# A gate's inner channels turned round on TensorE, and the gate's terms issued in another order, in the first layer of a two-layer image network

## The chip, the cores and the metric

One Trainium2 chip, of which the kernel uses one core. The metric is device time in microseconds (us) of one launch, which computes both layers for the whole batch of eight images. The kernel before takes 14973.04 us, the median of three runs (14967.72 to 14974.38). A core has five engines with instruction queues of their own: TensorE (PE; its weight loads are listed as PEld), VectorE (DVE), ScalarE (ACT), GpSimd (POOL) and SyncE (SP), which here only issues transfers (DMA). The engines work each in the order of its queue and wait for one another through semaphores.

## The reference, cut to what matters

The first layer, in which everything that the change touches lies, is this, for x of 8 images, 128 channels, 128 x 128 points. The second layer (a 3x3 convolution, a small scan over tokens, a group norm) is not touched.

```
feat = gelu(batchnorm(conv2d(x, conv_w, padding=3, dilation=3)))    # 64 channels
F2   = fft2(feat)
q = k = complex_l2_norm(F2 as 8 heads of 8 channels);  v = F2
attn = complex_softmax(einsum(q, conj(k)) * tau)                    # 8x8 per head
out_f = abs(ifft2(attn @ v))
cg   = gelu(batchnorm(conv2d(F2.real, cg1_w) + cg1_b))              # 64 -> MID = 4 channels
cg   = sigmoid(conv2d(cg, cg2_w) + cg2_b)                           # 4 -> 64 channels
gate = abs(ifft2(cg * F2))
x1   = concatenate([out_f, gate], channels) + x
```

Both convolutions of the gate have 1x1 kernels. So cg1_w, which mixes channels, may be applied to feat before the transform instead of to F2.real after it, and that is what the kernel does: it takes the 4 inner channels per image from feat and then transforms only these 4.

## The kernel before, in words

`network` runs `layer0` and then `layer1`. `layer0` goes over the batch in four pairs of images, p = 0 to 3. The 64 channels of image 0 lie on partitions 0 to 63 and those of image 1 on 64 to 127. For each pair it calls `convolve(p)` and then `spectral(p)`. A manual schedule keeps each engine's instructions in the order in which the program issues them.

`convolve` makes 6 rows of feat per group g. `combine(g)` forms sums and differences of input rows (tiles v), mostly on POOL. `block(g)` multiplies them on TensorE into four PSUM tiles m (line 276), which ScalarE copies (`low`, line 282) and VectorE adds up into feat; the Gelu of line 288 finishes the rows. In between, `turn(r)` takes four rows that an earlier group finished. Four transposes (line 307) put them into a PSUM tile tps, of which there are two buffers, and VectorE copies them into fT (line 308), where the 128 columns of the image lie on the partitions. Then four matmuls (line 312) make the gate's inner channels. In each the row of feat, 128 channels by 128 points, is the stationary side, and the moving side is cg1_w with 2 x MID = 8 columns (4 for each image, zero for the other image's channels). The result has the points on the partitions already, as fT has. After 16 rows (CH) VectorE copies 16 x 8 values to mT (line 315). `products(r)` (line 319) adds four rows to the Gram matrix of the softmax.

`spectral` begins with `rows(("m", b), mT, ...)`, `columns` and `hidden(b)`: the transform of the inner channels and their Gelu, kept in hid. After that come NP = 32 steps n of four channels each. For a step, `rows` (line 364) and `columns` (lines 373, 375) transform feat; `gated(n)` (lines 417 to 420, VectorE) multiplies with the gate cg into gp; `columns_back` (lines 427, 428, PSUM tile zps) and `rows_back` (line 436, then Abs, the sum with x on VectorE, and the store) transform back. The gate of step n is made in three parts: `gate_begin(n)`, four ScalarE instructions for the first inner channel (line 395); `gate_end(n)`, three products and three sums for the other inner channels (lines 405 and 408), on VectorE for n < 2 and otherwise on POOL; and `gate_close(n)`, the sigmoid on ScalarE (line 411). Tiles cg have three buffers. `softmax(k)` in three parts turns the Gram matrix into the matrix pT; its part 0 takes a root on ScalarE (line 495), its part 1 a transpose and an exponential (lines 500, 506), its part 2 another transpose (line 512). ScalarE loads a function table whenever it goes to a function of another set. `mixture`, from step 3 on, multiplies feat with pT for the other half of the output.

In the kernel before, the gates of steps 0 and 1 and part 0 of the softmax stand ahead of the loop, and in the loop the gate of step n + 2 is begun. The head of the loop reads:

```
gate_end(0); gate_close(0); softmax(0)
load_mixture(H - CH); load_mixture(H - 2 * CH)
gate_begin(1); gate_end(1)
for n in range(NP + 1):
    if n < NP:
        e = columns(n, 2)
        if n + 2 < NP:
            gate_begin(n + 2)
        gp = gated(n, e)
```

Of the kernel before, what the change touches and what calls it, by code (L numbers as in the profile page):

```python
# [9 lines left out]
F32 = mybir.dt.float32  # L10
# [6 lines left out]
P = 128  # L17
C = 128
H = 128
W = 128  # L20
# [3 lines left out]
MID = 4  # L24
# [117 lines left out]
def layer0(ctx, tc, x, w0, c0, x1):  # L142
# [9 lines left out]
    nc = tc.nc  # L152
# [9 lines left out]
    def cf(name):  # L162
        at, n = C0[name]
        return ct[:, at:at + n]

    def wf(name):
        at, n = W0[name]
        return wt[:, at:at + n]
# [52 lines left out]
        nc.vector.scalar_tensor_tensor(w_mid[:, k], convw[:, 3:6, :], half, w_sum, ALU.mult, ALU.add)  # L221
    w_four = (convw[:, 0:3, :], w_mid[:, 0], w_mid[:, 1], convw[:, 6:9, :])

    def convolve(p):

        with tc.tile_pool(name="l0_x", bufs=2) as xp, \  # L230
                tc.tile_pool(name="l0_v", bufs=1) as vp, \
                tc.tile_pool(name="l0_pc", bufs=1, space=PSUM) as pc, \
                tc.tile_pool(name="l0_pt", bufs=2, space=PSUM) as pt, \
                tc.tile_pool(name="l0_pm", bufs=1, space=PSUM) as pm:
            xins, vs, mps = {}, {}, {}
            FOUR = (1, 2, 0, 3)

            def load(g):

                if g == 0:  # L240
                    xins[0] = first_rows()
                    return
                lo = g * RW - 3
                n = min(RX, H - lo)
                xins[g] = []
                for b in range(2):
                    xt = xp.tile([P, RX, W], F32, name=f"xin{b}")
                    nc.sync.dma_start(xt[:, :n, :], x[2 * p + b, :, lo:lo + n, :])
                    if g < NW and n < RX:
                        nc.gpsimd.memset(xt[:, n:RX, :], 0.0)  # L250
                    xins[g].append(xt)

            def combine(g):
                for j in FOUR:
                    for b in range(2):
                        xt = xins[g][b]
                        v = vs[b, j] = vp.tile([P, 3, W], F32, name=f"v{b}{j}")
                        r0, r1, r2, r3 = (xt[:, 3 * k:3 * k + 3, :] for k in range(4))
                        eng = nc.vector if g == 0 and b == 0 else nc.gpsimd
                        if j == 1:  # L260
                            eng.tensor_add(v, r1, r2)
                        else:
                            eng.tensor_sub(v, *{0: (r0, r2), 2: (r2, r1), 3: (r1, r3)}[j])

            def columns_of(kx):
                dx = (kx - 1) * 3
                return max(0, -dx), min(W, W - dx), dx

            def block(g):
                m = {}  # L270
                for j in FOUR:
                    m[j] = pc.tile([P, 3, W], F32, name=f"m{j}")
                    for kx in (1, 0, 2):
                        wa, wb, dx = columns_of(kx)
                        for b in range(2):
                            nc.tensor.matmul(  # L276
                                m[j][b * CD:(b + 1) * CD, :, wa:wb], w_four[j][:, kx, :],
                                vs[b, j][:, :, wa + dx:wb + dx], start=(kx == 1), stop=(kx == 2))
                r = g * RW
                both = vp.tile([P, 2, 3, W], F32, name="both")  # L280
                low = vp.tile([P, 3, W], F32, name="low")
                nc.scalar.copy(low, m[2])
                nc.vector.tensor_add(both[:, 0], m[1], low)
                nc.vector.tensor_sub(both[:, 1], m[1], low)
                nc.vector.tensor_add(feat[:, r:r + 3, :], m[0], both[:, 0])
                nc.vector.tensor_sub(feat[:, r + 3:r + RW, :], both[:, 1], m[3])
                f = feat[:, r:r + RW, :]
                nc.scalar.activation(f, f, AF.Gelu, bias=bt, scale=bs)

            def rest():  # L290

                r, xt = NW * RW, xins[NW]
                m = pc.tile([P, 3, W], F32, name="m0")
                for ky in (1, 0):
                    for kx in (1, 0, 2):
                        wa, wb, dx = columns_of(kx)
                        for b in range(2):
                            nc.tensor.matmul(
                                m[b * CD:(b + 1) * CD, 0:H - r, wa:wb], convw[:, ky * 3 + kx, :],
                                xt[b][:, 3 * ky:3 * ky + H - r, wa + dx:wb + dx],  # L300
                                start=(ky == 1 and kx == 1), stop=(ky == 0 and kx == 2))
                nc.scalar.activation(feat[:, r:H, :], m[:, 0:H - r, :], AF.Gelu, bias=bt, scale=bs)

            def turn(r):
                tps = pt.tile([P, 4, P], F32, name="tps")
                for j in range(4):
                    nc.tensor.transpose(tps[:, j, :], feat[:, r + j, :], cf("ident"))
                nc.vector.tensor_copy(fT[:, r:r + 4, :], tps)
                if r % CH == 0:
                    mps[0] = pm.tile([P, CH, 2 * MID], F32, name="mps")  # L310
                for j in range(4):
                    nc.tensor.matmul(
                        mps[0][:, r % CH + j, :], feat[:, r + j, :], wf("cg1_w"), start=True, stop=True)
                if r % CH + 4 == CH:
                    nc.vector.tensor_copy(mT[:, r + 4 - CH:r + 4, :], mps[0])

            def products(r):
                for h in range(r, r + 4):
                    nc.tensor.matmul(gram, fT[:, h, :], fT[:, h, :], start=(h == 0), stop=(h == H - 1))

            for g in range(3):
                load(g)
            combine(0)
            turned = summed = 0
            for g in range(NW + 2):
                ready = min(H, g * RW)
                if g < NW:
                    block(g)
                elif g == NW:
                    rest()  # L330
                if g + 1 < NW:
                    combine(g + 1)
                if g + 3 <= NW:
                    load(g + 3)
                fresh = turned
                while turned + 4 <= ready:
                    turn(turned)
                    turned += 4
                while summed < fresh:
                    products(summed)  # L340
                    summed += 4
            while summed < turned:
                products(summed)
                summed += 4

    def spectral(p):

        with tc.tile_pool(name="l0_f1", bufs=1) as f1, \
# [50 lines left out]
            def gate_end(n):  # L399

                b, c = place(n)
                eng = nc.vector if n < 2 else nc.gpsimd
                for m in range(1, MID):
                    t = f2.tile([P, 4, NF], F32, name="cgt")
                    eng.tensor_mul(
                        t, hid[:, b, m:m + 1, :].broadcast_to([P, 4, NF]),
                        w2r[:, c:c + 4, m:m + 1].broadcast_to([P, 4, NF]))
                    eng.tensor_add(cgs[n], cgs[n], t)
# [113 lines left out]
            hidden(1)  # L522
            gate_end(0)
            gate_close(0)
            softmax(0)
            load_mixture(H - CH)
            load_mixture(H - 2 * CH)
            gate_begin(1)
            gate_end(1)
            for n in range(NP + 1):  # L530
                if n < NP:
                    e = columns(n, 2)
                    if n + 2 < NP:
                        gate_begin(n + 2)
                    gp = gated(n, e)
                    if n + 1 < NP:
                        b, c = place(n + 1)
                        rows(n + 1, fT, b * CD + c)
                if n > 0:
                    rows_back(n - 1)  # L540
                if n == NP:
                    break
                if n + 2 < NP:
                    gate_end(n + 2)
                if n >= START:
                    mixture()
                elif n > 0:
                    softmax(n)
                columns_back(n, gp)
                if n + 1 < NP:  # L550
                    gate_close(n + 1)
                if n >= START and n % 2 == 0:
                    mixture()
                roots()
                load_gate(n + 3)
                if n == NP - 5 and 2 * p + 2 < B:
                    first_load(p + 1)
# [603 lines left out]
```

## Time and profile before

| what | value |
|---|---|
| device time, median of three runs | 14973.04 us |
| device time of the profiled execution | 14973.45 us |
| span of the profiled execution | 14971.7 us, mean granted TensorE clock 0.986 |
| layer 0 within the span | about 0 to 2104 us, four pairs at intervals of 525.5 us |
| TensorE busy | 14356.8 us, 96% of the span |
| VectorE, ScalarE, POOL busy | 85%, 55%, 87% of the span |
| line 312, the gate's matmuls | 1024 records for 512 matmuls, mean 247 ns |
| line 307, transposes | 512 records, mean 284 ns |
| line 276, the convolution | 4032 records, about 480 ns |
| line 408 on POOL and on VectorE | 736 and 500 ns |
| line 405 on POOL and on VectorE | 628 and 424 ns |

The page lists busy times over the whole span, six sevenths of which belong to the second layer, so shares of it say little on the first. What follows reads single stretches: a timeline (start, length, engine, line, operation, output and inputs, shapes, count, and in brackets the idle time before it with what ended it), groups of instructions (busy time, mean ns of one, idle time before), and the chain of waits, which is followed back from the end of a stretch to whatever released each step. Ends of matmuls are modelled and overlap the next start, so that the step from start to start is the better price for one in a stream.

### The profile page before, as it was taken

To read this page: it belongs to the slowest core of one execution; us is meant where nothing else is said; L and a number is where in the kernel's file an instruction comes from. 1 tells how busy PE (TensorE), PEld (TensorE's weight loads), DVE (VectorE), ACT (ScalarE), POOL (GpSimd) and SP (SyncE) were. 2 spreads that over 40 slices of the span, in tenths; PEclk is the share of its full clock that TensorE was granted. 3 is DMA by queue.
4 is the path that set the end of the run, shared out by engine and by line. 5 is a ranking of instruction groups with operands and counts; after the bars stand their busy time and mean duration, and the time that the engine had idled before them with its cause. 6 is when DMAs were issued, how large, how long until landed. Compare 5 with 4: busy or idle time off the path is not lost.

```text
span 14971.7 us, 202160 instructions
## 1 busy us (share of the span) xinstructions
PE 14356.8 (96%) x71336; PEld 5692.1 (38%) x71336; DVE 12692.5 (85%) x12439; ACT 8275.3 (55%) x9202; POOL 12962.2 (87%) x7052
## 2 busy tenths in 40 slices
PE   9999999999999999999999999999999999999996
PEld 6676663333333333333333333333333333333332
DVE  3343359999999999999999999999999999999995
ACT  2354255555555555555555555555565555556553
POOL 5655659998999999999999999999999999999996
PEclk9999999999999999999999999999999999999996
DMA  3444456666666666666666666666666666666665
GB/s 126 148 121 119 128 119 121 119 119 118 129 138 133 137 131 137 136 133 134 133 138 134 135 133 134 138 134 135 133 135 138 131 136 134 136 133 135 136 133 138
DMA packets 1091891, 1976.10 MB, mean 132 GB/s; under 512 B 125760, under 2 KB 256832, under 8 KB 1082688
## 3 DMA queue, kind: packets, MB, share of 16 engines
q1 hardware_dynamic: 1090304, 1960.82, 60.7%
q8 instruction: 568, 9.31, 0.3%
q14 instruction: 443, 3.63, 0.1%
q10 hardware_dynamic: 576, 2.35, 0.0%
HBM read 419.16 MB, written 201.33 MB: 41 GB/s over the span
## 4 chain that ended last, share of the span: by engine, by line
PE 73%; DVE 18%; issue 4%; ACT 3%; DMA 1%; POOL 0%; DVEq 0%; SPq 0%; POOLq 0%; ACTq 0%
PE da L781 19%; PE yps L847 9%; PE ups L781 7%; PE pm L134 7%; DVE da L812 6%; PE m L276 4%; DVE h L820 4%; DVE h L796 4%; PE yps L853 4%; PE pm L733 4%; PE pm L866 3%; PE pm L745 3%; DVE hc L831 2%; PE da L726 2%; PE yps L837 2%
## 5 line engine op out<-in xcount | busy, mean ns | idle before, releaser
L826 POOL TENSOR_TENSOR hc<-h,cc 128x1024 f32<-128x1024 f32 x3584 | 8368.8, 2363 | 436.1 <-DVE h L820 418.0
L786 ACT ACTIVATE da<-da 128x1024 f32<-128x1024 f32 x3584 | 3618.9, 1010 | 4202.4 <-PE ups L781 2510.5
L796 DVE TENSOR_TENSOR h<-ups,bb 128x1024 f32<-128x1024 f32 x3584 | 4366.3, 1218 | 694.7 <-PE ups L781 313.9
L781 PE MATMUL da<-du,m_a 16*128 16x512 f32 x14336 | 4073.8, 645 | 139.0 <-DVE hc L831 134.9
L781 PE MATMUL ups<-du,m_u 16*128 16x512 f32 x14336 | 4119.1, 643 | 2.2 <-DVE h L796 1.3
L820 DVE TENSOR_TENSOR h<-da,h 128x1024 f32<-128x1024 f32 x2304 | 2820.7, 1224 | 79.1
L812 DVE TENSOR_TENSOR da<-da,h 128x1024 f32<-128x1024 f32 x2304 | 2819.8, 1224 | 6.6 <-ACT da L786 3.3
L134 PE MATMUL pm<-xin,l_wt 128*128 128x508 f32 (+1 forms) x4608 | 2414.4, 624 | 177.1 <-ACT xr L871 170.1
L818 POOL TENSOR_TENSOR h<-ah,h 128x1024 f32<-128x1024 f32 x768 | 1816.7, 2366 | 447.8 <-DVE ah L810 406.5
L781 PEld LDWEIGHTS da<-du,m_a 16*128 16x128 f32 x14336 | 1080.6, 184 | 2625.7 <-issue 1008.0
L847 PE MATMUL yps<-hc,l_ct 128*32 128x512 f32 x14336 | 1931.7, 611 | 0.0
L134 PEld LDWEIGHTS pm<-xin,l_wt 128*128 128x128 f32 x4608 | 751.9, 189 | 1621.4 <-issue 1396.4
L781 PEld LDWEIGHTS ups<-du,m_u 16*128 16x128 f32 x14336 | 1125.5, 184 | 379.9 <-DVE h L796 297.5
L786 ACT ACT_TABLE_LOAD x774 | 993.0, 1283 | 29.6 <-PE da L781 0.4
L810 DVE TENSOR_TENSOR ah<-da,h 128x1024 f32<-128x1024 f32 x768 | 932.0, 1214 | 0.0
L740 POOL TENSOR_TENSOR u<-dt,xc 128x512 f32<-128x512 f32 x512 | 653.7, 1277 | 187.0 <-ACT dt L735 187.0
L847 PEld LDWEIGHTS yps<-hc,l_ct 128*32 128x32 f32 x14336 | 283.8, 108 | 1375.8 <-issue 968.0
L735 ACT ACT_TABLE_LOAD x511 | 655.6, 1283 | 29.9 <-DMA cc<-bc 2.1
L803 POOL TENSOR_TENSOR cb<-bb,cc 128x512 f32<-128x512 f32 x512 | 654.2, 1278 | 13.0 <-DMA cc<-bc 13.0
L866 PEld LDWEIGHTS pm<-m_o,ym 128*128 128x128 f32 x4096 | 519.2, 192 | 318.7 <-issue 318.0
L831 DVE TENSOR_TENSOR hc<-da,hc 128x1024 f32<-128x1024 f32 x512 | 600.5, 1214 | 0.9 <-ACT da L786 0.8
L853 PE MATMUL yps<-xc,m_d 128*128 128x512 f32 x1024 | 582.7, 651 | 0.0
(175 smaller groups left out, 14709.8 us busy)
## 6 DMA issues: line engine op xcount, KB each, us to landing
bb<-bc SPq DMA_DIRECT2D x2048, 256.0 KB
cc<-bc SPq DMA_DIRECT2D x2048, 256.0 KB
du<-dt SPq DMA_DIRECT2D x2048, 64.0 KB
du<-u SPq DMA_DIRECT2D x2048, 64.0 KB
xin<-x SPq DMA_DIRECT2D x152, 768.0 KB
xin<-x SPq DMA_DIRECT2D x112, 640.0 KB
gn<-xr SPq DMA_DIRECT2D x256, 256.0 KB
v<-gn SPq DMA_DIRECT2D x256, 256.0 KB
```

What stands on the lines that cost most here:

```text
L134: nc.tensor.matmul(out[:, a:b, wa:wb], wt[:, t, :], src[:, r + dy + a - base:r + dy + b - base, wa + dx:wb + dx], start=(n == 0), stop=(n ...
L781: nc.tensor.matmul(o, w, v, start=True, stop=True)
L786: nc.scalar.activation(da, da, AF.Exp)
L796: nc.vector.tensor_mul(h, d["ups", s], state_row(i, "bb", s // GP))
L810: nc.vector.tensor_mul(d["ah"], da, before)
L812: nc.vector.tensor_mul(da, da, before)
L818: nc.gpsimd.tensor_add(h, d["ah"], h)
L820: nc.vector.tensor_add(h, d["da", s], h)
L826: nc.gpsimd.tensor_mul(hc, d["h", s], state_row(i, "cc", t))
L847: nc.tensor.matmul(d["yps"][g * DI:(g + 1) * DI], gather[:, t % LP, :], d["hc", GP * t + g // GP][:, g % GP], start=False, stop=(t in (3, ...
L853: nc.tensor.matmul(d["yps"], m_d, d["xc"][:, hf, :], start=False, stop=False, skip_group_check=True)
L866: nc.tensor.matmul(d["pm"][:, j, :], d["ym", hf][:, j * C:(j + 1) * C], m_of[:, hf, :], start=(hf == 0), stop=(hf == NH - 1))
```

## The change

The inner channels change sides. A new constant w_hid holds cg1_w in its first 8 columns and zeros in the other 24. After every 16 rows, `hidden_inputs` issues four matmuls with w_hid as the stationary side and four rows of feat (512 columns) as the moving side, each into its own 32 partitions of one PSUM bank. ScalarE copies the bank to ms. `hidden_back`, at the next turn or at the end of the convolution, transposes ms with four matmuls into a tps buffer, and VectorE copies the wanted 8 of every 32 columns into mT. In the spectral part only step 0's gate stays ahead of the loop. Steps 1 and 2 are begun and ended behind step 0's product, and each later step's gate is begun and ended behind a product too; step 1's `gate_end` goes from VectorE to POOL. Part 0 of the softmax moves into step 0.

```diff
+    w_hid = const.tile([P, 32], F32, name="w_hid")
+    nc.vector.memset(w_hid, 0.0)
+    nc.vector.tensor_copy(w_hid[:, 0:2 * MID], wf("cg1_w"))
...
                 nc.vector.tensor_copy(fT[:, r:r + 4, :], tps)
-                if r % CH == 0:
-                    mps[0] = pm.tile([P, CH, 2 * MID], F32, name="mps")
-                for j in range(4):
+                hidden_back()
+                if r % CH + 4 == CH:
+                    hidden_inputs(r + 4 - CH)
+
+            def hidden_inputs(r0):
+
+                mps = pm.tile([P, 4, W], F32, name="mps")
+                for q in range(4):
                     nc.tensor.matmul(
-                        mps[0][:, r % CH + j, :], feat[:, r + j, :], wf("cg1_w"), start=True, stop=True)
-                if r % CH + 4 == CH:
-                    nc.vector.tensor_copy(mT[:, r + 4 - CH:r + 4, :], mps[0])
+                        mps[32 * q:32 * q + 32], w_hid, feat[:, r0 + 4 * q:r0 + 4 * q + 4, :],
+                        start=True, stop=True)
+                ms = vp.tile([P, 4, W], F32, name="ms")
+                nc.scalar.copy(ms, mps)
+                waiting.append((r0, ms))
+
+            def hidden_back():
+                while waiting:
+                    r0, ms = waiting.pop()
+                    tps = pt.tile([P, 4, P], F32, name="tps")
+                    for j in range(4):
+                        nc.tensor.transpose(tps[:, j, :], ms[:, j, :], cf("ident"))
+                    nc.vector.tensor_copy(
+                        mT[:, r0:r0 + CH, :].rearrange("p (q j) m -> p j q m", j=4),
+                        tps.rearrange("p j (q k) -> p j q k", q=4)[:, :, :, 0:2 * MID])
...
                     products(summed)
                     summed += 4
+            hidden_back()
             while summed < turned:
...
-                eng = nc.vector if n < 2 else nc.gpsimd
+                eng = nc.vector if n == 0 else nc.gpsimd
...
             gate_close(0)
-            softmax(0)
             load_mixture(H - CH)
             load_mixture(H - 2 * CH)
-            gate_begin(1)
-            gate_end(1)
             for n in range(NP + 1):
                 if n < NP:
                     e = columns(n, 2)
-                    if n + 2 < NP:
-                        gate_begin(n + 2)
                     gp = gated(n, e)
+                    for k in (1, 2) if n == 0 else (n + 2,):
+                        if k < NP:
+                            gate_begin(k)
+                            gate_end(k)
...
-                if n + 2 < NP:
-                    gate_end(n + 2)
                 if n >= START:
                     mixture()
-                elif n > 0:
+                else:
                     softmax(n)
```

More of the change, by code (lines that the diff above doesn't have):

```diff
@@ L234, in convolve @@
                 tc.tile_pool(name="l0_pm", bufs=1, space=PSUM) as pm:
-            xins, vs, mps = {}, {}, {}
+            xins, vs, waiting = {}, {}, []
             FOUR = (1, 2, 0, 3)
```

## The prediction

> **What bounds the kernel now.** The page first: TensorE is the engine to shorten, but busy time is an average over two layers.
>
> ```profile
> PE 14356.8 (96%) x71336; PEld 5692.1 (38%) x71336; DVE 12692.5 (85%) x12439; ACT 8275.3 (55%) x9202; POOL 12962.2 (87%) x7052
> ```
>
> The change lies in layer 0 alone, the first 2,100 us (the first line-134 matmul is at 2108.70). The chain of waits there repeats every 525.5 us: a convolution of some 250 us, then a spectral part. I read the two separately, by engine, in order of time.
>
> Convolution: TensorE's timeline over one group of six rows (columns: start, length, engine, line). Starts count, since ends are modelled and overlap.
>
> ```profile
> 103.72 0.66 PE L307 MATMUL tps<-l_ct,feat 128*128 128x128 f32 x4
> 104.21 0.96 PE L312 MATMUL mps<-l_wt,feat 128*128 128x8 f32 x8
> 105.03 0.63 PE L307 MATMUL tps<-l_ct,feat 128*128 128x128 f32 x4
> 105.50 0.96 PE L312 MATMUL mps<-l_wt,feat 128*128 128x8 f32 x8
> 106.31 1.14 PE L319 MATMUL gram<-fT 128*128 128x128 f32 x8
> 107.38 4.03 PE L276 MATMUL m<-v,w_mid 128*64 128x384 f32 x24
> ```
>
> No idle is noted: TensorE alone sets this pace. VectorE, ScalarE and POOL are busy 30%, 14% and 68% in the window from 10 to 242 us. Start to start, a turn's four transposes take 0.48 us and its four gate matmuls 0.82 us (0.82 and 0.81), though they stream 8 columns each.
>
> ```profile
> L312 PEld LDWEIGHTS mps<-l_wt,feat 128*128 128x128 f32 x1024 | 124.4, 192 | 1.1
> L312 PE MATMUL mps<-l_wt,feat 128*128 128x8 f32 x1024 | 123.3, 247 | 0.0
> ```
>
> Weight load and matmul have as many records (two for an fp32 matmul): each of the 512 matmuls loads its own 128 columns of weights.
>
> Spectral part: from 300 to 510 us TensorE is busy 207.6 of 210 us, but only 38.8 of 49 us at the head (251 to 300). The chain of waits at the head says why:
>
> ```profile
> 263.06 1.28 ACT L411
> 264.36 0.42 ACT cg L411
> 264.80 1.28 ACT L495
> 266.09 0.20 ACT rn L495
> 266.29 1.34 ACT cg L395 x4
> 267.65 0.43 DVE cg L408
> ...
> 269.26 0.85 DVE cg L408
> 270.11 0.34 DVE gp L417
> ...
> 271.50 0.79 PE zps L427 x2
> ```
>
> The sigmoid for step 0 is ready at 264.78, but its product (gp, line 417) waits in VectorE's queue behind the softmax's root, which costs a table load on ScalarE, and behind step 1's gate. TensorE idles 4.75 us before 271.50.
>
> **What the Trainium skill says.** "TensorE: Matmul & The Clock Gate", section "LDWEIGHTS (loading the stationary operand)": a load costs by its columns, 128 here, whatever the rows. The trace agrees: 192 ns for a load of 128x128, 109 ns for one of 128x32. The same page, "Part 3: Packing small matmuls", says that matmuls of 32 output columns at partitions 0, 32, 64, 96 run side by side; line 847 below shows it. Its Part 1 says that an idle window of about 3.4 us halves the clock: after the 4.75 us of idle the granted clock is 0.50 (271 to 274 us). "TensorEngine Tiling (Array Packing)", "Key Properties": a change of tiling mode drains the array; line 847's price includes one.
>
> **The change, part by part.** All sums are per pair of images, then times four.
>
> *Removed gate matmuls*: 32 turns x 0.815 us = 26.1 us of TensorE, all on the path.
>
> *Added column-tiled matmuls*: per 16 rows, four 128x32-by-512 matmuls. Layer 1 has this shape:
>
> ```profile
> 3012.98 1.06 PE L847 MATMUL yps<-hc,l_ct 128*32 128x512 f32 x8
> 3013.97 1.13 PE L853 MATMUL yps<-xc,m_d 128*128 128x512 f32 x2
> ```
>
> A group of four costs 0.99 us: 8 x 0.99 = 7.9 us.
>
> *Added transposes*: 8 x 0.48 = 3.8 us.
>
> *Added ScalarE copy*: 8 of 128x512, as line 366's copy from PSUM, 0.58 us. ScalarE waits over 5 us per group, so its own time is nothing; its latency is paid only where TensorE comes for ms at once. VectorE's mT copy reads PSUM at a stride, which the trace lacks; the 292 ns of the old copy of 128 elements are a floor, a doubling would still hide under the 7.8 us of convolution that follow.
>
> *New waits of TensorE*, from the built program's order. (a) For r = 28 and 76, the gate matmuls, the next turn and the turn-back of ms share a group. In the group shown (its twin in order of work) ScalarE and VectorE do this:
>
> ```profile
> 104.45 1.03 ACT L288 ACTIVATE feat<-feat,bn_t,bn_s 128x768 f32<-128x768 f32 x1 [3.87 <-DVE feat L286]
> ```
> ```profile
> 104.42 0.69 DVE L308 COPY fT<-tps 128x512 f32<-128x512 f32 x1
> ```
>
> TensorE would do transposes 103.72 to 104.21, gate matmuls to 105.20, transposes to 105.69. ScalarE is in Gelu until 105.48, so the copy ends at about 106.05: TensorE waits 0.42 us with signalling. (b) At r = 20, 68 and 116 the order is transposes, ms transposes, transposes, and the third needs the first's PSUM buffer. VectorE reads that buffer 104.42 to 105.11; TensorE arrives at 104.68: 0.43 us. Queued behind both are the gram products and the next group's matmuls, all on the path: 2 x 0.42 + 3 x 0.43 = 2.1 us. (c) For the last 16 rows four gram products (0.94 us) stand between matmul and turn-back; signal to ScalarE 0.15 (ps to fa at 253.64), copy 0.58, signal back 0.06 (fa to er at 254.28) and the matmuls' modelled end 0.08 past their step make 0.87: nothing; without that cover 0.87 us. Bounds for the sum of waits: 0 (the conv's end shifts) and 8 x 0.9 = 7 us; I take 2.1.
>
> What is late next? POOL's sums for the following group: they end 10.0 us after a group's start, but only the last is needed 5.9 us after the next start; groups become 9.8 us at the shortest, so cover remains. Input DMAs: no queue of SP changes.
>
> Convolution: 26.1 - 7.9 - 3.8 - 2.1 = 12.3 us; x4 = **49 us**. Setting up w_hid: a memset and a 128x8 copy ahead of the first sums, about 0.15 us each by the smallest VectorE rows: 0.3 us, once.
>
> *Spectral head.* Step 0's product no longer waits. ScalarE: sigmoid done at 264.78, both steps' first terms (line 395, x8 in 2.75) to 267.5, fa copy to 268.0, table and root to 269.4, table and sigmoid of step 1 to 271.1. POOL takes step 1's six operations from VectorE: behind the first terms at 266.2, 3.6 us (0.63 and 0.74 each), done at 269.9, before ScalarE asks at 270.7; without that 0.8 us of cover, each further us of POOL would be paid. POOL then has step 2's 4.2 us, done at 274, needed at 278. VectorE: product of step 0 from 264.9 to 266.4, with the line-364 matmuls ending at 266.6; zps starts at 266.7 instead of 271.5, 4.8 earlier. With no idle window the clock may stay up: eight zps matmuls take 1.8 instead of 3.5 us. Then step 1's zps, before at 279.90, comes at 273.0 (clock up) or 275.0 (down): 6.9 or 4.9 us. The Exp, the sigmoid of step 2 and its product hang on TensorE's ops of step 0, and shift along; the 2.62 us wait for the softmax (line 512) stays. Later steps have the same order on every engine. For the four pairs, starting from each one's own clock, I get 6.9, 6.0, 6.0, 5.4: **24 us**; bounds 19 and 28.
>
> Sum: 14973.45 (profiled; its span is 14971.7) - 49 - 24 + 0.3 = 14900.7; the median of the runs shown is 0.4 lower. Prediction 14900.
>
> **Rivals.**
> (1) *The head's gain is eaten*: step 1's sigmoid becomes late, as POOL's step-1 and step-2 terms or ScalarE's table loads take the place of the old wait. For it: POOL is slower (1.37 against 0.85 us a term), two tables load in a row. Against: the 0.8 us of cover, and 98.9% TensorE afterwards. 14973 - 49 = 14924.
> (2) *Every turn-back exposes copy and transposes*: the waits are 7 us a pair or more, the group costs line 847's 1.07 us. Convolution gain 26.1 - 8.6 - 3.8 - 7 = 6.7, x4 = 27; with the head 14922; and with half a head, 14934.
> (3) *Slower: the four column groups run one after another*, as all read the same weights. Price: a 512-column fp32 matmul steps 0.86 us (line 466), so 3.46 a group; per pair 26.1 - 8 x (3.46 + 0.48) - 2.1 = -7.5, x4 = +30; minus the head's 24: 14979. It decides from 3.28 us a group on. Against: line 847 also has equal weights for its four, and takes 0.99.
> (4) *The change doesn't do what it says*: the scheduler keeps the old order. The built program's lists show the new order on all five engines, so 14973 gets next to nothing.
>
> **How the numbers follow.** Forecast 0.80 (14880 to 14920); rival 1 0.09, rival 2 0.07, rival 3 0.03, rival 4 0.01. The range reaches to 14928 to hold rival 1 and most of 2; its lower end has no waits in the convolution (8 us less), the head's 28 (4 less), and no half clock after the wait at line 512, where zps and er lose some 2.3 us a pair now (9 less). 0.2%, about what a measurement can tell from no change, is 30 us, 14943: faster 0.94, same 0.04, slower 0.02.
>
> **What would show it.** Right: line 312's rows become four-column-group matmuls of about 1.0 us per 16 rows; TensorE idle of about 0.4 us at five places a pair; the period of 525.5 falls to about 507; zps of step 0 follows the line-364 matmuls without idle, and the clock there is near 1. Wrong: groups near 3.4 us; idle before ms transposes at all eight places; a sigmoid of step 1 waiting on POOL; or layer 1, which is unchanged, taking another time than 12,870 us.

## The result, and the profile after

The changed kernel takes 14888.74 us (median of 5 runs, 14886.39 to 14897.05) against 14967.72 for the kernel before in the same comparison: 79 us or 0.53% less. The ratio of the runs is 0.9951, 95% interval 0.9939 to 0.9962; it fits their means, which lie 73 us or 0.49% apart. The profiled execution took 14897.05 us with a span of 14895.3, 76.4 less than the profiled execution before.

The first matmul of the second layer (line 134) divides a span into its layers. It starts at 2108.70 us before and at 2032.03 after: the first layer lost **76.7 us**. The second took 12863.0 and 12863.3 us. The page hardly shows it; TensorE's share stays at 96%.

```profile
PE 14287.1 (96%) x70696; PEld 5588.1 (38%) x70696; DVE 12683.2 (85%) x12417; ACT 8294.9 (56%) x9234; POOL 12983.2 (87%) x7076
```

TensorE's timeline over a group of six rows that has everything in it, the counterpart of the group shown before (start, length, engine, line, operation, tiles, shapes, count):

```profile
77.16 0.66 PE L311 MATMUL tps<-l_ct,feat 128*128 128x128 f32 x4
77.75 1.07 PE L321 MATMUL mps<-feat,w_hid 128*32 128x512 f32 x8
78.75 0.66 PE L311 MATMUL tps<-l_ct,feat 128*128 128x128 f32 x4
79.52 0.65 PE L333 MATMUL tps<-l_ct,ms 128*128 128x128 f32 x4
80.01 1.06 PE L340 MATMUL gram<-fT 128*128 128x128 f32 x8
81.00 4.04 PE L280 MATMUL m<-v,w_mid 128*64 128x384 f32 x24
```

The four column groups of 16 rows take 1.00 us from start to start, where four turns of the old kernel took 3.26. Between the last two transposes there is a gap: 78.75 plus 0.49 is 79.24, but the transposes of ms start at 79.52, when ScalarE's copy is through:

```profile
78.88 0.59 ACT L325 COPY ms<-mps 128x512 f32<-128x512 f32 x1
```

The other wait stands in a group where the transposes of ms come second (the bracket gives the idle time before a piece and what ended it):

```profile
141.93 0.60 PE L333 MATMUL tps<-l_ct,ms 128*128 128x128 f32 x4
142.87 0.66 PE L311 MATMUL tps<-l_ct,feat 128*128 128x128 f32 x4 [0.35 <-DVE fT L312]
```

At the head of the spectral part TensorE now goes from the line-386 matmuls (line 364 before) into zps without a gap. First TensorE and then ScalarE, whose last sigmoid here is that of step 1:

```profile
249.04 0.71 PE L395 MATMUL er<-fa,l_ct 128*128 128x260 f32 x2 [1.39 <-ACT hid L406]
...
250.87 1.81 PE L386 MATMUL ps<-l_ct,fT 128*128 128x128 f32 x8
252.52 0.39 PE L449 MATMUL zps<-l_ct,gp 128*128 128x128 f32 x2
...
258.70 0.45 PE L449 MATMUL zps<-l_ct,gp 128*128 128x128 f32 x2
```
```profile
250.63 2.75 ACT L417 ACTIVATE cg<-hid,l_wt 128x65 f32<-128x65 f32 x8
253.28 0.56 ACT L388 COPY fa<-ps 128x512 f32<-128x512 f32 x1
253.87 1.28 ACT L517 ACT_TABLE_LOAD   x1
255.16 0.20 ACT L517 ACTIVATE rn<-rn 128x1 f32<-128x1 f32 x1
255.38 1.28 ACT L433 ACT_TABLE_LOAD   x1
256.67 0.42 ACT L433 ACTIVATE cg<-cg 128x260 f32<-128x260 f32 x1
```

The table below takes starts from TensorE's timelines. "Convolution" is the stretch from a pair's first convolution matmul to its first ps matmul from mT. "Spectral" goes on to the next pair's first convolution matmul (for the fourth pair to line 134). "Mixture" is the first mixture matmul, counted from that ps matmul, as are the times of zps further down; behind the first mixture matmul every kernel here has the same order on each engine. All in us, for the four pairs.

| kernel | convolution | spectral | mixture |
|---|---|---|---|
| before | 243.2, 243.0, 243.1, 243.2 | 281.9, 282.4, 282.3, 281.4 | 45.2, 45.6, 45.6, 43.6 |
| after | 229.8, 229.8, 229.8, 229.9 | 274.3, 275.3, 275.2, 279.4 | 37.6, 38.5, 38.5, 41.7 |

The convolution gave 53.3 us in the four pairs and the spectral part 23.7. The sum is 77.0, against 76.7 for line 134; the difference is a start of the first convolution matmul that is 0.4 later.

The fourth pair gained only 2.0 us in its spectral part. Up to zps of step 0 its head shows the same order and the same three idle stretches as the first pair's, but the rows of er take 0.87 us from start to start where the first pair's take 0.44: half clock. The first pair's rows, then the fourth's:

```profile
246.63 0.60 PE L395 MATMUL er<-fa,l_ct 128*128 128x260 f32 x2
247.07 0.59 PE L397 MATMUL er<-fa,l_ct 128*128 128x252 f32 x2
```
```profile
1761.03 1.07 PE L395 MATMUL er<-fa,l_ct 128*128 128x260 f32 x2
1761.90 1.04 PE L397 MATMUL er<-fa,l_ct 128*128 128x252 f32 x2
1764.33 1.23 PE L395 MATMUL er<-fa,l_ct 128*128 128x260 f32 x2 [1.39 <-ACT hid L406]
```

The stretches' table (each engine's busy time, its instructions in brackets, then TensorE's granted clock) for 4 us of the first pair's head and of the fourth's:

```profile
248.00:252.00 4.00, 2.96 (x14) 2.76 (x15) 1.79 (x5) 3.97 (x11) 0.26 (x1) 1.00 0.77 170
1762.00:1766.00 4.00, 2.61 (x7) 1.63 (x6) 0.86 (x2) 2.99 (x7) 0.61 (x1) 0.50 0.96 205
```

### The profile page after: what moved, and what is told of

Same layout as the page of the kernel before. It is cut to its first block, busy times and chain, and to the rows that moved or that the text cites. A ratio compares the mean times of both kernels' runs of the same rounds, so it can differ in the third digit from the quotient of the medians.

```text
span 14895.3 us, 200912 instructions
## 1 busy us (share of the span) xinstructions
PE 14287.1 (96%) x70696; PEld 5588.1 (38%) x70696; DVE 12683.2 (85%) x12417; ACT 8294.9 (56%) x9234; POOL 12983.2 (87%) x7076
## 4 chain that ended last, share of the span: by engine, by line
PE 72%; DVE 18%; issue 4%; ACT 4%; DMA 1%; POOL 0%; SPq 0%; DVEq 0%; POOLq 0%; ACTq 0%
PE da L800 19%; PE yps L866 9%; PE ups L800 7%; PE pm L134 7%; DVE da L831 6%; PE m L280 4%; DVE h L839 4%; DVE h L815 4%; PE yps L872 4%; PE pm L752 4%; PE pm L885 3%; PE pm L764 3%; DVE hc L850 2%; PE da L745 2%; PE yps L856 2%
```

## The experiments

Where a run has no interval, the layer-0 end (the start of line 134) is compared. It repeats to 0.6 us for the changed kernel (2032.03 and 2031.46) while the second layer, the same code in every kernel here, took between 12846.7 and 12871.4 us in the profiled executions. Single times are therefore worth less than these traces. Between different kernels, the parts of the first layer whose code is the same differ by up to some 2 us over the four pairs, by 4 in one case below, so that a smaller gain is not read from one trace.

### The two parts by themselves

`conv_only` has the diff's lines in `convolve` and w_hid, with `spectral` as before; `head_only` has the diff's lines in `spectral`, with `convolve` as before.

> The convolution's part of the change alone (inner channels with the weights as stationary side), the spectral part as before. Theory (both parts work, each on its own path): the time from a pair's first convolution matmul to its first ps matmul from mT falls by 13.2 us a pair as in the changed kernel, the spectral part keeps its 282 us; 53 us less in all, about 0.35%. Rival (the head's new order gave the convolution its gain, or hid a loss of it): less than 40 us.

Measured: 14923.02 against 14966.81 (ratio 0.9972, 0.9962 to 0.9982). Its layer-0 end is at 2053.83, 54.9 us earlier; convolution 230.5, 229.8, 229.3, 230.0; spectral 281.8, 279.9, 281.2, 283.0. The convolutions give 53.0 us, as expected; the other 2 lie in the spectral parts, whose code is unchanged. The medians of the runs differ by only 44. In the profiled execution the unchanged second layer was 8.4 us longer than in before's, which may be the reason; the interval, 27 to 57 us, holds both.

> The spectral head's new order alone, the convolution as before. Theory: 24 us less in all (between 19 and 28, as the half clock falls), about 0.16%; zps of step 1 comes about 20.4 us after the first ps matmul from mT where TensorE keeps full clock, up to 23.6 where it doesn't, against 26.9 to 28.9 before. Rival (the head's gain needs the shorter convolution): under 10 us.

Measured: 14942.22 against 14966.81 (0.9987, 0.9980 to 0.9993). The layer-0 end is at 2089.01, 19.7 us earlier, near the lower end of what was expected, and 18.6 of it in the spectral parts; mixture at 41.7, 40.4, 39.7, 39.7; zps of step 1 at 23.6, 23.0, 22.7, 22.8. So each part works without the other: 54.9 + 19.7 = 74.6 of the 76.7 us. But no head had full clock throughout here; in the first one the granted clock is 0.50 from 263 to 266 us:

```profile
263.00:266.00 3.00, 2.62 (x6) 2.17 (x7) 0.45 (x2) 2.97 (x8) 0.00 (x0) 0.50 0.02 5
```

### The two halves of the head

Both keep the convolution of before.

```diff
 # softmax_only, against before
-            softmax(0)
...
-                elif n > 0:
+                else:
                     softmax(n)
```
```diff
 # gate_only, against the changed spectral part
             gate_close(0)
+            softmax(0)
...
-                else:
+                elif n > 0:
                     softmax(n)
```

> Of the head's new order, only part 0 of the softmax moves into step 0; step 1's gate stays on VectorE ahead of the loop. Convolution as before. The root's table load (1.28 us) and root leave ScalarE's way to step 1's first terms, and VectorE's way to the product. Theory: zps of step 0 starts about 1.4 us earlier than before (18.7 us after the first ps matmul from mT, against 20.1), some 6 us in all. Rival (the softmax was the whole wait): 4.8 us earlier a pair, 20 us or more in all.

Measured: zps of step 0 at 17.6, 18.6, 18.6, 18.6 against 20.1, 20.1, 19.9, 19.2, on average 1.5 earlier; layer-0 end 2097.37, 11.3 us earlier. The mechanism at zps of step 0 is the one expected, not the whole wait of 4.8; the sum is twice the expected one. 9.2 us of it lie in the spectral parts, where step 1's zps came 2.3 us earlier on average, and 2.0 in the convolutions, whose code is unchanged. Why step 1 gained more than step 0 was not followed further.

> Of the head's new order, only step 1's gate goes behind step 0's product and to POOL; part 0 of the softmax stays ahead of the loop. Convolution as before. VectorE's product still waits for the root (to 266.3 in the old trace's times). Theory: zps of step 0 starts about 3.2 us earlier than before (16.9 us after the first ps matmul from mT), zps of step 1 about 5 us earlier, some 20 us in all. Rival (POOL's slower terms make step 1's sigmoid late): zps of step 1 less than 3 us earlier, with ScalarE's sigmoid of step 1 waiting for POOL.

Measured: zps of step 0 at 15.8, 16.8, 16.8, 16.8, zps of step 1 at 22.1, 22.9, 23.1, 23.0 (before 28.5, 28.9, 28.9, 26.9: 5.5 earlier on average); layer-0 end 2090.66, 18.0 us earlier. As expected, the gate carries most of it. The halves are not additive: 18.0 + 11.3 is more than the 19.7 of both. Both shorten the same queue of VectorE, so that the gains overlap; how much of the rest TensorE's half clock takes was not tested.

### Are the column groups what saves time?

```diff
 # serial, against the changed kernel
-    w_hid = const.tile([P, 32], F32, name="w_hid")
+    w_hid = const.tile([P, 4, P], F32, name="w_hid")
...
-    nc.vector.tensor_copy(w_hid[:, 0:2 * MID], wf("cg1_w"))
+    for q in range(4):
+        nc.vector.tensor_copy(w_hid[:, q, 32 * q:32 * q + 2 * MID], wf("cg1_w"))
...
-                        mps[32 * q:32 * q + 32], w_hid, feat[:, r0 + 4 * q:r0 + 4 * q + 4, :],
-                        start=True, stop=True)
+                        mps, w_hid[:, q], feat[:, r0 + 4 * q:r0 + 4 * q + 4, :],
+                        start=(q == 0), stop=(q == 3))
```

> As the changed kernel, but w_hid has four sets of 128 columns, each with cg1_w in its own 32 columns and zeros elsewhere, and the four matmuls of 16 rows add up in the whole bank: the same result from four full-width matmuls, which cannot run side by side. Theory (the convolution's gain rests on the four column groups running at once): a group of four goes from about 1.0 to 3.4 us, the convolution part from 229.8 to about 248.5 us a pair, longer than before the change (243.1); some 75 us more in all than the changed kernel. Rival (the gain comes from the stationary side being loaded less often, 32 loads a pair instead of 128, whatever its width): the convolution part stays below 235 us.

Measured: 14961.27 us; layer-0 end 2099.25, 67.2 us later than the changed kernel; convolution 249.3, 248.0, 248.0, 248.0. TensorE's timeline of one group:

```profile
105.25 3.60 PE L322 MATMUL mps<-feat,w_hid 128*128 128x512 f32 x8
108.68 1.05 PE L341 MATMUL gram<-fT 128*128 128x128 f32 x8
```

3.43 us instead of 1.00, for the same four matmuls of 512 columns. So the theory holds: with full-width matmuls the turned-round channels would have cost 5 us a pair more than the old form. That is rival 3 of the prediction in its real size; the changed kernel avoids it because the groups do run at once. (The convolutions alone are 74.0 us longer. All four first mixture matmuls came at 37.6 here, 6 us in all earlier than in the changed kernel, which is why the total is 67.)

### The waits that the change brought, and idle time in the head

```diff
 # late_back, against the changed kernel
                 nc.vector.tensor_copy(fT[:, r:r + 4, :], tps)
-                hidden_back()
...
                 while summed < fresh:
                     products(summed)
                     summed += 4
-            hidden_back()
+                hidden_back()
```

> As the changed kernel, but ms is transposed back after the group's gram products instead of right behind a turn's transposes; nothing else moves. Theory: the five waits of TensorE a pair (0.28 us twice for ms, 0.45 us three times for a PSUM buffer) go, the convolution part falls from 229.8 to 227.9 us a pair, 7.6 us in all. Rival (the idle moves to the next thing that TensorE needs, a PSUM buffer of the next group): the convolution part stays above 229 us.

Measured: 14874.9 us; convolution 227.0, 227.1, 227.3, 227.4, 2.6 us less a pair; layer-0 end 2018.09, 13.9 us earlier than the changed kernel. 10.5 of these lie in the convolution. The group shown above has no gap left before the transposes of ms (78.16 plus 0.89 is 79.05):

```profile
77.67 0.66 PE L311 MATMUL tps<-l_ct,feat 128*128 128x128 f32 x4
78.16 1.06 PE L339 MATMUL gram<-fT 128*128 128x128 f32 x8
79.05 0.60 PE L332 MATMUL tps<-l_ct,ms 128*128 128x128 f32 x4
```

The theory holds, with 0.7 us a pair more than the waits I had counted. The rest, 3.4 us, is almost all in the heads, where only the first pair's was held back (mixture 40.3, 37.6, 37.6, 37.6).

```diff
 # gram_fill, against late_back
+                lag = 4 if g == NW - 1 else 8 if g >= NW else 0
...
-                while summed < fresh:
+                while summed < fresh - lag:
...
-            while summed < turned:
+            while summed < H - 8:
...
             rows(("m", 0), mT, 0)
+            products(H - 8)
             hidden(0)
             rows(("m", 1), mT, MID)
             gate_begin(0)
             rows(0, fT, 0)
             hidden(1)
+            products(H - 4)
```

> As late_back, and the last eight rows' gram products (two of 0.94 us) are left to the spectral head, where TensorE waits 0.80 and 1.39 us for ScalarE. Theory of the clock (these idle stretches decide whether the head runs at half clock): convolution part 226.0 us, first mixture matmul at most 0.2 us later after the first ps matmul from mT than at full clock now (37.6), and no pair at 41 us or more. Rival (the half clock comes from elsewhere): the pairs still lie between 37.6 and 41.7.

Measured: 14865.49 us; convolution 226.4, 225.9, 225.1, 225.8; mixture 38.6, 37.2, 38.6, 36.8; layer-0 end 2010.48. The work fits into the idle stretches as expected, and no pair is at 41. But two mixtures come 1.0 us later than 37.6, where at most 0.2 was expected, and three pairs are still at half clock for part of the head (zps of step 0 at 15.2, 15.2 and 15.1 instead of 14.2). So the theory of the clock fails: the idle stretches do not decide it. In the fourth pair the rows of er run at half pace although no idle stretch longer than 0.67 us stands before them in the head:

```profile
1742.51 2.02 PE L386 MATMUL ps<-l_ct,fT 128*128 128x128 f32 x8 [0.67 <-ACT fa L388]
1744.37 0.93 PE L395 MATMUL er<-fa,l_ct 128*128 128x260 f32 x2
1745.08 1.05 PE L397 MATMUL er<-fa,l_ct 128*128 128x252 f32 x2
1745.92 1.91 PE L366 MATMUL gram<-fT 128*128 128x128 f32 x8
```

> The changed kernel once more, for its clock and its unchanged second layer. Theory (each pair's head falls into one of a few patterns of full and half clock, by chance): convolution part 229.8 us in every pair as before; the first mixture matmul of a pair between 37.5 and 41.8 us after the first ps matmul from mT, in another mix than 37.6, 38.5, 38.5, 41.7. Rival (the fourth pair is slow by its place in the program): again three pairs at 38.6 or less and the fourth at 41 or more.

Measured: 14886.15 against 14965.08 (0.9947, 0.9934 to 0.9961). The mixture matmuls come at 37.58, 38.52, 38.52, 41.71 us. The first execution had 37.59, 38.53, 38.54, 41.72. My theory of chance is wrong: the pattern repeats to 0.02 us. The second layer took 16.6 us less than in the first execution (12846.7 against 12863.3), so nearly all of the difference between these two executions lies there.

> The kernel of gram_fill, timed against the changed kernel on the same chip. From the traces' first layers: 21 us less than the changed kernel (16 of them in the convolution, 5 in the head by its clock); 14868 us.

Measured: 14869.57 (0.9937, 0.9922 to 0.9953), 16.6 us less than the changed kernel on that chip, layer-0 end 2010.03, 21.4 less. Mixture at 38.5, 37.2, 38.5, 36.8, once more the pattern of its first execution.

### Moving the softmax further back

TensorE's longest idle stretch in the changed head is 3.04 us before the softmax's second transpose (line 534; 2.62 before the change).

```diff
 # soft_late, against gram_fill
                 if n >= START:
                     mixture()
-                else:
-                    softmax(n)
                 columns_back(n, gp)
+                if n < START:
+                    softmax(n)
```

> As gram_fill, and the parts of the softmax come behind columns_back in a step instead of ahead of it, so that TensorE does step 2's zps (1.8 us at full clock) before it waits for the softmax's second transpose. Theory: the 3.04 us of idle at that transpose shrink by 1.8 us and the half clock behind it goes (2.3 us): the first mixture matmul comes 2 to 4 us earlier, 8 to 16 us in all against gram_fill; against the changed kernel some 22 us less in all. Rival (VectorE and ScalarE set that place: part 1 starts later and the transpose with it): the first mixture matmul comes within 0.5 us of gram_fill's.

Measured: 14873.34 (0.9936, 0.9923 to 0.9950); mixture at 41.2, 41.8, 42.8, 42.0; layer-0 end 2024.89, 14.4 us later than gram_fill. The idle stretch at line 534 did shrink to 1.96 us, but two new ones came before zps of steps 1 and 2 (1.20 and 2.27 us). Both theories missed that. ScalarE's timeline shows the cause: the sigmoid of step 1 stands behind the root, which now waits for VectorE, and that of step 2 behind the exponential.

```profile
253.17 0.20 ACT L517 ACTIVATE rn<-rn 128x1 f32<-128x1 f32 x1 [1.26 <-DVE rn L516]
253.39 1.28 ACT L433 ACT_TABLE_LOAD   x1
254.69 0.42 ACT L433 ACTIVATE cg<-cg 128x260 f32<-128x260 f32 x1
...
261.75 0.31 ACT L528 ACTIVATE gm<-gm 128x128 f32<-128x128 f32 x1 [3.06 <-DVE gm L527]
262.07 1.28 ACT L433 ACT_TABLE_LOAD   x1
263.37 0.42 ACT L433 ACTIVATE cg<-cg 128x260 f32<-128x260 f32 x1
```

```diff
 # soft_end, against soft_late
                 columns_back(n, gp)
-                if n < START:
-                    softmax(n)
                 if n + 1 < NP:
                     gate_close(n + 1)
+                if n < START:
+                    softmax(n)
```

> As gram_fill, but the parts of the softmax come behind the sigmoid of the next step's gate, at the end of a step. Theory (in soft_late the product of a step waited for the sigmoid, and the sigmoid in ScalarE's queue behind the softmax's root or exponential; the softmax itself is needed only at step 3): step 2's zps comes about 26.4 us after the first ps matmul from mT instead of 29.9, TensorE waits about 1 us instead of 3 for the softmax's second transpose, the first mixture matmul comes at about 34 us instead of 37 to 38.5; 14 us less in all than gram_fill. Rival (each later place of the softmax makes the head longer, as soft_late showed): the first mixture matmul at 41 us or more.

Measured: 14857.85 us (14854.87 to 14862.72) against 14965.08, a ratio of 0.9929 (0.9916 to 0.9941): the fastest of all, 28 us less than the changed kernel in the same comparison. Layer-0 end 2004.88; mixture at 37.5, 36.6, 37.5, 38.4; step 2's zps at 29.1, 28.1, 29.1, 29.1. Better than gram_fill, but by 5 us in the first layer and not by 14, and 4.0 of these lie in the convolutions, whose code is the same in both. There the clock differs: in the second pair, after a wait of 4.42 us in both kernels, the granted clock over the first 4 us of the convolution is 0.65 here and 0.50 in the second execution of gram_fill, and TensorE reaches its first transposes 1.5 us sooner. The spectral parts gained only 1.1 us. Of the theory, the part on the sigmoids holds: step 2's zps has no wait before it. But the wait at line 534 is still 1.97, and step 1's zps is later, at 22.8, behind 1.38 us of idle. VectorE's timeline names the new wait: the reciprocal behind the root (line 518), with step 1's product (line 439) queued behind it. It is the old wait of the head, one step later.

```profile
254.26 0.16 DVE L518 RECIPROCAL rn<-rn 128x1 f32<-128x1 f32 x1 [1.34 <-ACT rn L517]
254.45 0.73 DVE L519 TENSOR_SCALAR gm<-gm,rn 128x128 f32<-128x128 f32 x1
255.10 0.42 DVE L439 TENSOR_TENSOR gp<-er,cg 128x260 f32<-128x260 f32 x1
```

```diff
 # soft_split, against soft_end
                     nc.scalar.activation(rn, rn, AF.Sqrt)
+                elif k == 1:
                     nc.vector.reciprocal(rn, rn)
                     nc.vector.tensor_scalar(gm, gm, rn, None, ALU.mult)
-                elif k == 1:
```

> As soft_end, but the reciprocal and the scaling that need the softmax's root go from the end of step 0 to the end of step 1 (VectorE), behind step 1's product. Theory (in soft_end step 1's product waits in VectorE's queue behind these two, which wait for the root): TensorE's 1.38 us of idle before step 1's zps go, it comes 21.3 us after the first ps matmul from mT instead of 22.7; the first mixture matmul up to 1.4 us earlier a pair, 4 to 6 us less in all. Rival (the wait moves on to the softmax's transposes, now later in the chain): the first mixture matmul no earlier than in soft_end (36.6 to 38.4).

Measured: 14866.72 against 14956.28 (0.9935, 0.9921 to 0.9948); layer-0 end 2008.60. Step 1's zps does come at 21.2 us and without a wait, but the mixture stays at 37.5, 37.5, 38.4, 37.5: the rival is right. TensorE's timeline has the wait at the softmax's first transpose instead (line 522):

```profile
259.53 0.33 PE L522 MATMUL pf<-l_ct,gm 128*128 128x128 f32 x1 [1.55 <-DVE gm L520]
```

## Why the prediction was right, and where a term was off

The predicted time, 14900, is 11 us above the measured median, and 79 us moved where 73 were forecast. By the prediction's own steps:

- **Removed and added matmuls.** The convolution fell by 13.3 us a pair, not 12.3. The added work took 8 x 1.00 us plus 0.10 us for each group that follows transposes (0.59 from transposes to group, 0.49 between other pieces), close to the 0.99 taken from line 847. The mis-sized term is the removed one: it had been priced by its own step of 0.82 us, but the gram products behind the old matmuls were longer too, 1.07 us for eight records against 0.98 and 0.99 behind transposes now. Over the second pair's convolution their steps fall from 32.1 to 31.0 us, which is the 1 us a pair. So 53.3 us came from the four convolutions where 49 were told.
- **Waits.** In number and place as told, 0.28 us twice (0.42 told) and 0.50 three times (0.94 from start to start less 0.44; 0.43 told): 2.1 us a pair, as in the sum. `late_back` removes them and gives 2.6.
- **The turn-back's copy.** VectorE's strided copy takes 285 ns, below the 292 that was meant as a floor; it is hidden.
- **Head.** 24 us told, 23.7 measured in the spectral parts. The sum is right, its working only in part. The order of events is as told: product of step 0 from 250.75, zps without a gap, sigmoid of step 1 on ScalarE at 256.67, POOL's six operations through at 255.79, with 0.9 us of cover (0.8 told). But the step "starting from each one's own clock" failed. The first three pairs gained 7.6, 7.1 and 7.1 us (6.9, 6.0 and 6.0 told), the fourth 2.0 (5.4 told): the head has a clock pattern of its own under the new timing, which two executions repeat. That the sum fits is luck, as the errors cancel.
- **Rivals.** Rival 1 (the head's gain eaten) is refuted by `head_only` and `gate_only`; the wait that it feared, a late sigmoid of step 1, shows up only in `soft_late`, where the sigmoid stands behind the softmax's root. Rival 2's full exposure did not happen. Rival 3 is what `serial` builds: +5 us a pair (+7.5 told), decided by the groups running at once. Rival 4 fell with the timeline.
- **The median** fell 2 to 3 us more than the profiled executions. With 25 us between the second layer's fastest and slowest execution here, that is no finding. From line 134 on the second layer takes 12,863 us before and after; the prediction's 12,870 for it, and the 2104 us for the first layer's end in the table before, are rough, but neither stands in the sum.

## What to carry to other kernels

When a small product streams few columns against a large stationary side, turn it round: sixteen matmuls per 16 rows, each with its own 128 stationary columns and only 8 streamed, cost 3.26 us, four 32-column groups side by side 1.00, even with 0.44 us of transposes to undo the turn; without the column groups it would have been a loss. In an in-order queue, put what the bound engine needs next ahead of what is needed three steps later, and then look at every queue the moved work lands in: the softmax moved back three times here, and each time its wait came back on another engine's queue.

## What the runs showed of the hardware

- TensorE's half clock came without a long idle stretch before it. In the fourth pair's head of the changed kernel the rows of er run at half pace from 1761.03, and up to there the longest stretch is 0.80 us. The first pair has the same stretches (0.80, 0.68, 1.39 us) at a granted clock of 1.00. In gram_fill's fourth pair the granted clock is 0.57 from 1744 to 1748 us, in which TensorE was busy throughout. The prediction had leaned on "TensorE: Matmul & The Clock Gate", Part 1, by which an idle window of about 3.4 us halves the clock; that alone does not account for these traces. What sets the phase stays open: two executions of the changed kernel, and two of gram_fill, repeat their patterns to 0.04 us, which speaks for the program's own timing and against chance.
- The four column groups have the same number of weight loads and matmul records as the four full-width matmuls of `serial` (256 each in the first layer), loads of 108 instead of 190 ns, and take 1.00 us against 3.43.
- Unchanged code had a spread of 25 us: the second layer's 12846.7 to 12871.4 us. What moves it was not tested.
